# Full-width products of the attention stage issued as four 32-column groups where the array is already tiled

## The chip, the cores and the metric

One core of one Trainium2 chip runs the whole program in one launch. The metric is the device time of that launch in microseconds, the median of the runs shown. All operands are float32.

## What is computed

The input is 8 images of 256 channels by 32 x 32 places. Layer 0 is a convolutional attention, layer 1 is a plain attention and a mixture of 8 experts. Cut to what matters:

```python
# layer 0, on a group-normalised image, 8 heads of 32 channels
q = einsum('bchw,oc->bohw', x, q_w)                  # 1024 queries for each image
k, v = pooled and layer-normed maps of kv_w @ x      # 1426 keys: levels 32x32, 16x16, 11x11, 5x5, each + 3x3 depthwise
out = softmax(q k^T * 32**-0.5) v                    # for each head
x = x + proj_w @ (out mixed by an 8-head global token) + proj_b
# layer 1, on tokens of 256 channels
t = t + softmax((ln(t) Wq)(ln(t) Wk)^T / 16) (ln(t) Wv)
# experts: 8 of them, three products of 256 x 256 each, gates from the mean over the batch
t = t + sum_e gate_e * (relu(bn(relu(bn(ln(t) W1_e)) W2_e)) Wo_e + bo_e)
```

## The kernel before

**Stages.** `attention` does layer 0 and, beside it, layer 1; `experts` does the rest. The attention stage is one loop of 384 steps: 8 images, 2 groups of 4 heads (`c`), 2 halves of the queries and 12 chunks of up to 128 keys (`kc`). The profile shows the first step's scores at about 79 us and the last products at 1970 us.

**One step.** `scores` issues four products of 32 rows, one for each head, which lie in four row groups of TensorE's array and write the four banks of the one buffer `sc`. ScalarE takes the exponential of all 128 x 2048 numbers into `pt` (6 buffers). `values`, for the chunk one step earlier, issues four products whose stationary side is 32 columns wide, in four column groups of the array; they write the four quarters of the partitions of `pv`. In every second step a DMA that accumulates adds one `pt` to another, and VectorE adds such pairs up for the softmax sums; `sums` multiplies them by ones, again in four column groups of 32 (`sm<-pt,con` in the profile).

**Background.** All other work of the stage runs as generators between the steps: key and value maps of the next image (`sm<-xi,kvw`, `sm<-xl,kvw`), queries (`xi,qw`), transposes of keys and values by tokens (`con,acc`, `con,kt`), the projection (`att,mt`), and all of layer 1 (`t,gw`, `y,t`, `wv,t`, `p,v`, sums by `s,con`). Most of these products have a stationary side of 128 x 128 and a moving side of 256, 402 or 512; they write the small buffers `sm` or `sx` of one bank each. After each step's `values`, `f.step((PACE, PACE1))` lets generators put such products on TensorE.

**The order.** `Flow` records every instruction through its `Engine` wrappers. All of them pass through the line `ins = fn(*args, **kwargs)` (L669), which is why the profile has one line for nearly everything and one goes by tiles. Each engine runs strictly in the order of recording. Which generator goes next comes from a planner: `note` adds up a cost for each instruction on a clock for each engine, and `runnable` compares these clocks with the times at which tiles become ready. For TensorE the planner keeps the form of the array in `self.tiled` ("rows", "columns" or None for the full array) and adds an amount to its clock when the form changes:

```python
tiling = None if op == "transpose" else self.tiling(srcs)
if tiling != self.tiled:
    cost += {None: 0.09, "rows": 0.2, "columns": 0.13}[tiling]
    self.tiled = tiling
```

So an ordinary step goes through the array forms rows (`sc`), columns (`pv`), full (background), and again rows.

Of the kernel before, what the change touches and what calls it, by code (L numbers as in the profile page):

```python
# [16 lines left out]
P = 128  # L17
# [3 lines left out]
DH = 32  # L21
# [30 lines left out]
class Kit:  # L52


    def __init__(self, nc):
        self.nc = nc
        self.n = 0
# [80 lines left out]
def chain(*gens):  # L138
    for g in gens:
        yield from g  # L140
# [515 lines left out]
class Flow:  # L656
# [4 lines left out]
    class Engine:  # L661
# [3 lines left out]
        def __getattr__(self, op):  # L665
            fn = getattr(self.eng, op)

            def call(*args, **kwargs):
                ins = fn(*args, **kwargs)  # L669
                self.flow.note(self.name, op, ins, args, kwargs)  # L670
                return ins

            return call

    def __init__(self, tc, kit):
        nc = tc.nc
        self.tc, self.kit = tc, kit
        self.now = dict.fromkeys(("PE", "DVE", "ACT", "POOL", "SP"), 0.0)
        self.last = {}
        self.ready, self.read, self.writer, self.reader, self.slots, self.open = {}, {}, {}, {}, {}, set()  # L680
        self.pe = self.Engine(self, "PE", nc.tensor)
        self.ve = self.Engine(self, "DVE", nc.vector)
        self.act = self.Engine(self, "ACT", nc.scalar)
        self.pool = self.Engine(self, "POOL", nc.gpsimd)
        self.sp = self.Engine(self, "SP", nc.sync)
        self.threads = []
        self.cut = {}
        self.also = {}
        self.tiled = None
        self.credit, self.port = [0.0, 0.0], 0.0  # L690

    def tile(self, pool, shape, tag, bufs=1):
# [18 lines left out]
    def cost(self, engine, op, out, ins):  # L711
# [26 lines left out]
            return 0.14 + 0.00065 * n  # L738
        return 0.15 + 0.00107 * n

    @staticmethod
    def tiling(ins):

        rows, columns = ins[0].shape[0], ins[0].shape[-1]
        return "columns" if columns <= DH and rows > 8 else "rows" if rows == DH else None

    def note(self, engine, op, ins, args, kwargs):
        aps = [a for a in (*args, *kwargs.values()) if hasattr(a, "tensor") or hasattr(a, "space")]
        out = kwargs.get("out", args[0] if args else aps[0])
        srcs = [a for a in aps if a is not out]  # L750
        prev = self.last.get(engine)
        if prev is not None:
            self.tc.add_manual_dep(
                ins.ins,
                prev,
                mybir.DependencyInfo(mybir.DependencyClass.NoSync, mybir.DependencyReason.DATA),
                reason="program order",
            )
        self.last[engine] = ins.ins.name
        start = self.now[engine]  # L760
        names = [n for a in srcs for n in self.keys(a)]
        outs = self.keys(out)
        for n in (*names, *outs):
            if self.writer.get(n) != engine:
                start = max(start, self.ready.get(n, 0.0))
        for o in outs:
            if self.reader.get(o, engine) != engine:
                start = max(start, self.read.get(o, 0.0))
        cost = self.cost(engine, op, out, srcs)
        if engine == "PE":  # L770

            tiling = None if op == "transpose" else self.tiling(srcs)
            if tiling != self.tiled:
                cost += {None: 0.09, "rows": 0.2, "columns": 0.13}[tiling]
                self.tiled = tiling

        wide = [a for a in srcs if a.space != PSUM and a.free_size() > 4]
        if "dma" not in op and engine == "POOL" or engine == "DVE" and wide and (len(wide) > 1 or op in ("tensor_scalar", "tensor_copy")):
            start = max(start, self.port)
            self.port = start + cost  # L780
        self.now[engine] = end = start + cost
        lag = 0.15
        if "dma" in op:
            size = 4e-3 * out.shape[0] * out.free_size() if out.space != DRAM else 4e-3 * srcs[0].shape[0] * srcs[0].free_size()
            lag = 2.0 + 0.0045 * size if engine == "SP" else 1.5 + 0.0078 * size
        for n in {*outs, self.key(out)}:
            self.ready[n] = max(self.ready.get(n, 0.0), end + lag)
            self.writer[n] = "DMA" if "dma" in op else engine
        self.open.difference_update(names)
        for n in {*names, *map(self.key, srcs)}:  # L790
            self.read[n] = max(self.read.get(n, 0.0), end + lag)
            self.reader[n] = engine
# [88 lines left out]
def attention(tc, kit, f, outer, ended, nb, consts, x, t1, t2, hn, bounds, vecs, q_t, kv_t, proj_t, gqk_t, wqk, wqkv, vecs1, w1_d, w1c, gate_d, wrc, vecs2, bnvec):  # L881
# [6 lines left out]
    with ExitStack() as ctx:  # L888
# [5 lines left out]
        def T(pool, shape, tag, bufs=1):  # L894
            return f.tile(pool, shape, tag, bufs=bufs)
# [567 lines left out]
        def scores(b, c, sl, kc):  # L1463
            k0, w = KEY_CHUNKS[kc]
            t = T(psum, [P, 4, 512], "sc")
            for j in range(4):
                r = slice(DH * j, DH * j + DH)
                f.pe.matmul(t[:w, j, :], lhsT=ks[b, c][r, k0 : k0 + w], rhs=qs[b, c][r, sl], start=True, stop=True)
            pt = T(work, [P, 4, 512], "pt", bufs=6)
            f.act.activation(pt[:w], t[:w], AF.Exp, scale=SCALE0)  # L1470
            return pt

        def values(b, c, kc, pt, pv):
            w = KEY_CHUNKS[kc][1]
            for j in range(4):
                h = 4 * c + j
                f.pe.matmul(
                    pv[DH * j : DH * j + DH, :],
                    lhsT=vts[b][kc // 4][:w, kc % 4, h * DH : (h + 1) * DH],
                    rhs=pt[:w, j, :],  # L1480
                    start=kc == 0,
                    stop=kc == NKC - 1,
                )

        def add(kc, pt, into):

            w = KEY_CHUNKS[kc][1]
            f.pool.dma_start(
                out=into[:w].rearrange("p j q -> p (j q)"), in_=pt[:w].rearrange("p j q -> p (j q)"), accum_op=ALU.add
            )  # L1490
# [305 lines left out]
        def unit(b, c, sl, n, pairs):  # L1796
            rec = yield from sums(n, pairs)
            yield from normalise(b, c, sl, rec, n)
            normalised[0] += 1
            if c and sl.start:  # L1800
                f.spawn(project(b), 1)
# [7 lines left out]
        f.finish(lambda: key_parts[0] > 0)  # L1809
        f.spawn(chain(mix(), weights1(), outputs()), 5)  # L1810
        f.spawn(layer1(), 6)
        steps = [(b, c, half, kc) for b in range(nb) for c in range(2) for half in range(2) for kc in range(NKC)]

        pts = {}
        for i in range(len(steps) + 1):
            if i < len(steps):
                b, c, half, kc = steps[i]
                sl = slice(half * 512, half * 512 + 512)
                if kc % 4 == 0:
                    f.finish(lambda: key_parts[0] > 3 * b + kc // 4)  # L1820
                if (half, kc) == (0, 0):
                    f.finish(lambda: (b, c) in qs and (b or (c, 0) in asked))
                    turn[0] = 2 * b + c
                    atts[b, c] = T(work, [P, HW], "att", bufs=2)
                if i == 4:
                    f.finish(lambda: {0, 1}.issubset(whole))
                if b == 0 and kc == 0:
                    f.finish(lambda: (c, half) in asked)
                pts[i] = scores(b, c, sl, kc)
                f.step()  # L1830
            if i:
                b1, c1, half1, kc1 = steps[i - 1]
                if kc1 == 0:
                    pv = T(psum, [P, 512], "pv")
                    pairs = []
                    sl1 = slice(half1 * 512, half1 * 512 + 512)
                    f.spawn(unit(b1, c1, sl1, i // NKC, pairs), 0)
                f.finish(lambda: kc1 // 4 in vts[b1])
                values(b1, c1, kc1, pts[i - 1], pv)
                if kc1 % 2:  # L1840
                    add(kc1, pts.pop(i - 1), pts[i - 2])
                    pairs.append(pts.pop(i - 2))
                if kc1 == NKC - 1:
                    f.finish(lambda: projected[0] >= b1)
                    f.act.activation(atts[b1, c1][:, sl1], pv, AF.Copy)
            if i < len(steps):
                f.step((PACE, PACE1))
        f.finish(lambda: projected[0] == nb)
        f.also.clear()
        f.finish(lambda: f.free("sx") < NEVER)  # L1850
# [683 lines left out]
```

## Time and profile before

| what | us |
|---|---|
| three timed runs | 3314.24, 3327.75, 3323.16 |
| their median | 3323.16 |
| profiled execution, span | 3321.6 |
| TensorE matmuls busy in that span | 3135.7 (94%) |
| weight loads busy | 1914.5 (58%) |
| VectorE busy | 2449.7 (74%) |
| ScalarE busy | 1734.7 (52%) |
| GpSimd busy | 1204.5 (36%) |

The profile gives of its execution the span alone, from the first to the last instruction; this lies 1.6 us under the median of the timed runs. In the groups of instructions `sc<-q,kn 32*128 32x512` reads: the tile `sc` is written from the tiles `q` and `kn`, the stationary side has 32 rows and 128 columns, the moving side is 32 x 512. A float32 product appears as two passes, that is two loads (PEld) and two matmuls (PE). A transpose appears as one. The durations of matmuls overlap and their ends are modelled, so that the distances between starts are the better measure. In the timeline a row is one group of equal instructions: start, length, engine, what, count.

### The profile page before, as it was taken

To read this page: it belongs to the slowest core of one execution; us is meant where nothing else is said; L and a number is where in the kernel's file an instruction comes from. 1 tells how busy PE (TensorE), PEld (TensorE's weight loads), DVE (VectorE), ACT (ScalarE), POOL (GpSimd) and SP (SyncE) were. 2 spreads that over 40 slices of the span, in tenths; PEclk is the share of its full clock that TensorE was granted. 3 is DMA by queue.
4 is the path that set the end of the run, shared out by engine and by line. 5 is a ranking of instruction groups with operands and counts; after the bars stand their busy time and mean duration, and the time that the engine had idled before them with its cause. 6 is when DMAs were issued, how large, how long until landed. Compare 5 with 4: busy or idle time off the path is not lost.

```text
span 3321.6 us, 43017 instructions
## 1 busy us (share of the span) xinstructions
PE 3135.7 (94%) x15970; PEld 1914.5 (58%) x15970; DVE 2449.7 (74%) x4066; ACT 1734.7 (52%) x2328; POOL 1204.5 (36%) x1303
## 2 busy tenths in 40 slices
PE   8687899999999999899899998999999999999997
PEld 4332244344344345345344355777888888888886
DVE  5687788786887886986884555445878887787776
ACT  4476666576576576576566543334333334444442
POOL 2211413213213214213211112006755566777775
PEclk9798999999999999999999999999999999999999
DMA  2357656656646646656556656224444440000000
GB/s 75 84 122 165 125 105 147 130 101 157 130 99 157 138 101 147 137 115 130 125 116 129 143 115 244 73 83 163 142 152 146 146 141 25 20 20 32 20 13 21
DMA packets 112428, 368.09 MB, mean 111 GB/s; under 512 B 13696, under 2 KB 39048, under 8 KB 88976
## 3 DMA queue, kind: packets, MB, share of 16 engines
q0 software_dynamic: 28608, 179.85, 28.2%
q1 hardware_dynamic: 80240, 183.42, 15.9%
q8 instruction: 128, 2.10, 0.3%
q10 hardware_dynamic: 3360, 1.97, 0.2%
q14 instruction: 92, 0.75, 0.1%
HBM read 115.60 MB, written 84.45 MB: 60 GB/s over the span
## 4 chain that ended last, share of the span: by engine, by line
PE 60%; DVE 3%; issue 3%; ACT 2%; DMA 2%; POOL 2%; SPq 0%; DVEq 0%; POOLq 0%; ACTq 0%
PE bank L669 20%; PE sm L669 13%; PE y L669 10%; PE sc L669 6%; PE sx L669 6%; PE pv L669 5%; ACT pt L669 2%; DVE h L669 1%; DMA pt<-pt 1%; DVE u L669 1%; DVE c L669 1%; POOL t L669 0%; ACT h L669 0%; DMA hn<-hn 0%; POOL tm L669 0%
## 5 line engine op out<-in xcount | busy, mean ns | idle before, releaser
L669 ACT ACTIVATE pt<-sc 128x2048 f32<-128x2048 f32 (+1 forms) x384 | 720.2, 1875 | 324.3 <-PE sc L669 270.0
L669 DVE SCALAR_TENSOR_TENSOR acc<-p,vec,acc 128x225 f32<-128x225 f32 (+7 forms) x928 | 527.8, 576 | 29.1 <-ACT acc L669 4.7
L669 PE MATMUL sc<-q,kn 32*128 32x512 f32 (+1 forms) x3072 | 444.7, 649 | 96.5 <-ACT pt L669 95.4
L669 DVE TENSOR_TENSOR pt<-pt,pt 128x1024 f32<-128x1024 f32 x320 | 386.8, 1252 | 142.2 <-DMA pt<-pt 130.3
L669 POOL DMA_DIRECT2D pt<-pt x192 | 174.0, 907 | 778.7 <-ACT pt L669 625.7
L669 PE MATMUL pv<-pt,vt 128*32 128x512 f32 (+1 forms) x3072 | 419.9, 619 | 0.0
L669 ACT ACTIVATE h<-h,bnvec 128x512 f32<-128x512 f32 x456 | 344.9, 805 | 63.8 <-DVE h L669 51.9
L669 ACT ACTIVATE p1c<-bank 128x256 f32<-128x256 f32 x228 | 87.4, 383 | 556.1 <-PE bank L669 538.8
L669 POOL TENSOR_TENSOR rstd<-rstd,mhalf 128x4 f32<-128x4 f32 (+2 forms) x88 | 107.0, 1216 | 672.3 <-DVE rstd L669 618.3
L669 DVE TENSOR_TENSOR h<-p1c,bank 128x512 f32<-128x512 f32 x228 | 155.4, 682 | 213.5 <-PE bank L669 208.3
L669 PEld LDWEIGHTS sc<-q,kn 32*128 32x128 f32 (+1 forms) x3072 | 116.2, 178 | 286.1 <-ACT pt L669 186.0
L669 POOL TENSOR_TENSOR tm<-h,tm 128x256 f32<-128x256 f32 x206 | 239.0, 1160 | 16.2
L669 DVE TENSOR_TENSOR h<-u,bank 128x256 f32<-128x256 f32 x456 | 232.2, 550 | 7.9
L669 PEld LDWEIGHTS pv<-pt,vt 128*32 128x32 f32 (+1 forms) x3072 | 60.8, 108 | 300.7 <-issue 288.4
L669 POOL TENSOR_TENSOR tm<-h 128x512 f32<-128x512 f32 x103 | 134.2, 1303 | 194.3 <-ACT h L669 192.2
L669 DVE TENSOR_TENSOR h<-h,gate 128x1024 f32<-128x1024 f32 x128 | 200.5, 1566 | 1.6 <-DMA h<-h 1.2
L669 PE MATMUL bank<-h,w2e 128*128 128x256 f32 (+1 forms) x612 | 199.0, 454 | 1.9 <-DVE h L669 1.9
L669 PE MATMUL y<-t,s3e 128*128 128x256 f32 x768 | 187.0, 379 | 2.3 <-POOL t L669 2.3
L669 PE MATMUL bank<-t,s1e 128*128 128x256 f32 x750 | 182.4, 379 | 0.0
L669 PE MATMUL sm<-y,t 128*128 128x256 f32 x752 | 180.6, 385 | 0.0
L669 POOL TENSOR_TENSOR t<-h 128x512 f32<-128x512 f32 x106 | 137.3, 1295 | 106.3 <-DVE h L669 87.5
L669 DVE TENSOR_TENSOR u<-h,bank 128x512 f32<-128x512 f32 x228 | 156.8, 688 | 24.2 <-PE bank L669 0.5
(316 smaller groups left out, 5619.2 us busy)
## 6 DMA issues: line engine op xcount, KB each, us to landing
pt<-pt POOLq DMA_DIRECT2D x160, 1024.0 KB, 7.4
h<-h SPq DMA_DIRECT2D x130, 512.0 KB, 3.4
xi<-in_x_dram SPq DMA_DIRECT2D x16, 512.0 KB, 6.3
t<-t SPq DMA_DIRECT2D x8, 1024.0 KB, 9.3
res<-t SPq DMA_DIRECT2D x32, 256.0 KB, 3.9
t<-res SPq DMA_DIRECT2D x32, 256.0 KB, 4.6
hn<-res SPq DMA_DIRECT2D x32, 256.0 KB, 2.9
hn<-hn SPq DMA_DIRECT2D x16, 512.0 KB, 4.7
```

The costliest lines, as they stand in the source:

```text
L669: ins = fn(*args, **kwargs)
```

## The change

While the attention loop runs (`f.columns`), a matmul whose stationary side is 128 x 128 and whose moving side has at least 128 columns is issued as four matmuls, each with 32 columns of the stationary side, the whole moving side, and 32 partitions of the output, if the instruction recorded last on TensorE left the array in rows or columns. Transposes do not pass through this branch, stay full width, and set the form to full, so that products which follow a transpose stay full width as well until the next tiled product. The planner's amount for going to the full array changes from 0.09 to 0.2. The rest of the kernel is as it was.

```diff
@@ Flow.Engine.__getattr__
-            return call
+            if op != "matmul":
+                return call
+
+            def product(out, lhsT, rhs, **kwargs):
+                if not self.flow.narrow(lhsT, rhs):
+                    return call(out, lhsT=lhsT, rhs=rhs, **kwargs)
+                for j in range(0, P, DH):
+                    call(out[j : j + DH], lhsT=lhsT[:, j : j + DH], rhs=rhs, **kwargs)
+
+            return product
@@ Flow.__init__
         self.tiled = None
+        self.columns = False
@@ Flow
+    def narrow(self, lhsT, rhs):
+
+        return self.columns and self.tiled is not None and tuple(lhsT.shape) == (P, P) and rhs.free_size() >= P
@@ Flow.note
             if tiling != self.tiled:
-                cost += {None: 0.09, "rows": 0.2, "columns": 0.13}[tiling]
+                cost += {None: 0.2, "rows": 0.2, "columns": 0.13}[tiling]
                 self.tiled = tiling
@@ attention
         f.spawn(layer1(), 6)
+        f.columns = True
         steps = [(b, c, half, kc) for b in range(nb) for c in range(2) for half in range(2) for kc in range(NKC)]
...
             if i < len(steps):
                 f.step((PACE, PACE1))
+        f.columns = False
         f.finish(lambda: projected[0] == nb)
```

## The prediction

> **What bounds the kernel now.** I read first the page's busy shares and slices, then the table by stretches of time, then TensorE's waits, and last its timeline inside the attention stage.
>
> ```profile
> PE 3135.7 (94%) x15970; PEld 1914.5 (58%) x15970; DVE 2449.7 (74%) x4066; ACT 1734.7 (52%) x2328; POOL 1204.5 (36%) x1303
> ...
> PE   8687899999999999899899998999999999999997
> ```
>
> One row of the table by stretches, then the first row of TensorE's waits (us in total, times, longest):
>
> ```profile
> 480.00:760.00 280.00, 270.20 (x1526) 125.62 (x1526) 227.23 (x394) 179.02 (x221) 66.51 (x75) 0.99 0.58 125
> ```
>
> ```profile
> PE sc L669 <- ACT pt L669: 95.4, 95, 3.3
> ```
>
> TensorE is busy nearly everywhere. In the stretch from 480 to 760 us (columns: PE, PEld, DVE, ACT, POOL busy, then clock, DMA share, GB/s) it is busy for 96.5% at a clock of 0.99; VectorE follows at 81%, ScalarE at 64%. The only wait of size is `sc` for the exponential, 95 us in 95 places. Going through the 383 steps of the loop, 67 of the 68 steps with neither background product nor transpose wait there, and of the 265 steps that hold a full-width background product 245 hold no TensorE wait at all. So a step with background work is as long as its TensorE work, and the question is what TensorE spends there beside streaming. TensorE's timeline (start, length, count of records):
>
> ```profile
> 682.21 1.14 PE L669 MATMUL sc<-q,kn 32*128 32x512 f32 x8
> 683.28 1.06 PE L669 MATMUL pv<-pt,vt 18*32 18x512 f32 x8
> 684.27 1.62 PE L669 MATMUL sm<-xl,kvw 128*128 128x402 f32 x4
> 685.73 1.89 PE L669 MATMUL sm<-wv,t 128*128 128x256 f32 x8
> 687.55 1.14 PE L669 MATMUL sc<-q,kn 32*128 32x512 f32 x8
> 688.62 1.06 PE L669 MATMUL pv<-pt,vt 128*32 128x512 f32 x8
> 689.62 0.66 PE L669 MATMUL sx<-con,acc 128*128 128x128 f32 x4
> 690.11 1.04 PE L669 MATMUL sm<-con,acc 128*128 128x128 f32 x8
> 691.08 1.14 PE L669 MATMUL sc<-q,kn 32*128 32x512 f32 x8
> 692.15 1.07 PE L669 MATMUL pv<-pt,vt 128*32 128x512 f32 x8
> 693.03 1.04 PE L669 MATMUL sx<-pt,con 128*32 128x512 f32 x8
> 694.00 1.09 PE L669 MATMUL sm<-con,acc 128*128 128x128 f32 x8
> ...
> 703.18 1.99 PE L669 MATMUL sx<-y,t 128*128 128x256 f32 x8
> 705.10 1.14 PE L669 MATMUL sc<-q,kn 32*128 32x512 f32 x8
> ```
>
> Read the distances between starts; over the whole stage they repeat within a few ns, and I give the medians.
> - **Leaving columns.** `pv` takes 0.996 us when a full-width group follows (688.62 to 689.62) and 0.883 when another column group follows (692.15 to 693.03): 0.113 us for the switch.
> - **Entering full.** Eight passes of 256 take 1.924 us to the next `sc` after `pv` (703.18 to 705.10) and 1.820 after another full-width group (685.73 to 687.55): 0.104 us. Transposes pay less: four take 0.492 after `pv` (689.62 to 690.11), 0.437 after a full-width group: 0.055.
> - **Leaving full.** Full-width passes of 256 follow each other every 0.216 us, eight are 1.728, so 1.820 holds 0.092 for the switch to rows.
> - **Streaming is the same in both forms.** A pass of 512 takes 0.429 us full width, and four column groups together take 0.429 for each of their passes (`sx<-pt,con`). Splitting neither saves nor adds streaming, if all four run side by side.
>
> **What the Trainium skill says.** "TensorEngine Tiling (Array Packing)", Key Properties: changing the tiling mode, not just the tile, drains the engine. The trace agrees: 0.09 to 0.11 us for each leaving. The same page, Restrictions, rules out float32 transposes under column tiling; the trace shows them at 128*128 alone, so the switches around them stay. "TensorE: Matmul & The Clock Gate", LDWEIGHTS: a load takes its columns divided by 1.2, in ns, so 107 ns for 128 and 27 for 32. The trace agrees: successive loads of 128 start 107 ns apart, which is the 0.104 of entering, and the first pass of `pv` is 25 ns longer than its later ones.
>
> **The change part by part.** *What is split.* In the changed program's order of TensorE instructions 1178 products are split: 852 with 256 moving columns, 54 with 402, the others with 512 (four of the 256s lie behind the last `sc`). That is 3534 more matmuls, each two loads and two matmul records. No other engine gets an instruction for it; 382 switches from rows to columns stay.
>
> *Switches that vanish and that come.* Counted in the two orders (before, after), groups of columns with few rows taken as columns:
> - columns to full 240, 10, at 0.113 + 0.104: 52.1 and 2.2 us
> - full to rows 243, 33, at 0.092: 22.4 and 3.0
> - columns to transposes 76, 92, at 0.113 + 0.055: 12.8 and 15.5
> - columns to rows 72, 281, at 0.113: 8.1 and 31.8
>
> The sum falls from 95.4 to 52.5 us, **by 43 us**. For one ordinary step: 0.113 + 0.104 + 0.092 before, 0.113 after, so 0.196 us of 3.99.
>
> *What of it is on the path.* Nearly all, as 245 of 265 steps are TensorE's alone. In the other 20 (7.5%) the gain only makes a wait longer: 3.2 us back. A dense step falls from 3.99 to 3.79 us and stays above the 3.14 us of a step that waits for ScalarE.
>
> *Splitting itself.* The trace before has no column group with 256 moving columns. From below: no cost, as in `sx<-pt,con` after `pv`, whose loads are under way while `pv` still streams; a gain is excluded because the passes already stream at full rate. From above: each product shows its first 32-column load, 0.025 us x 1178 = 29 us. I take nothing; the cover is the pass before, 216 ns long against four loads of 27.
>
> *The planner.* The new amounts change the order on every engine. Of small-buffer work, 5.6 us of TensorE time moves from behind the last `sc` into the stage; work only moved costs nothing on a bound engine. In the experts stage 104 instead of 112 products of 512 and 14 more of 256 stand on TensorE: 8 x 0.858 less 14 x 0.432, 0.9 us less. Which steps get which products is reshuffled; steps that wait now lose 134 us in all in the loop, and I allow 8 us either way for that. The `pt` transfers on GpSimd's queue (7.4 us to land) get a step 5% shorter; VectorE waits for them 120 us today, and late ones would show as ScalarE waiting for a `pt` buffer, today 22 us.
>
> Sum: 3321.6 - 43.0 + 3.2 - 0.9 = 3280.9 us for the profiled execution. It stood 1.6 us under the median, so **3283 us** (-1.2%).
>
> **The rivals.**
> *Issue cannot keep up (slower).* A split 256-wide pass needs four load-and-matmul pairs in 216 ns, one each 54 ns; before it was one each 216. With R ns for a pair, each such pass takes 4R where 4R exceeds 216. The gain of 43 us is gone at 852 x 2 x (4R - 216) = 43 us, R = 60 ns, and the kernel is slower by over 0.5% from R = 63 on. The densest chain before (`sc`, `pv`, `sx<-pt,con`: 24 pairs in 2.9 us) is one pair each 122 ns, set by streaming, so a sustained rate in question is not shown. "TensorE: Matmul & The Clock Gate", Back-to-back issue gap, gives 81 ns as sustained for such pairs at 128 columns: then 1704 x 108 ns = 184 us more, less 43, **3464 us**. Against it: that figure is for loads of 128 columns, and in one column group the records of the four pairs start 7 ns apart, which needs them waiting in the queue, but also says that they are accepted that fast. Also the blocks of 256 instructions (16 KB each) come in 0.9 to 1.5 us by the queue's packets, while a block will last 7 us at the densest. Chance 7%.
>
> *Another resource takes half.* The exponential, the `pt` transfers or VectorE (83% busy after) end more steps, or the loads of each product show: gain 43 - 21, **3302 us**. For it: 120 us of VectorE waits for `pt`. Against it: these waits lie beside a busy TensorE. Chance 12%, of which 5% within 0.5%.
>
> *The change does little, as the planner's order spends the gain*: 3318 us. Against it: the counts above are of the order as built. Chance 2%.
>
> **How the numbers follow.** About 0.5% (17 us) is what a measurement of this kernel can tell from no change, so faster means under 3306. The forecast has 79%, the rivals as above. Faster: 79 + 7 = 86%; same: 5 + 2 = 7%; slower 7%. Range: the upper bound of the unknown split cost (3283 + 29 = 3312) and the half-gain case lie below 3312; the lower end allows 8 us for order and as much for steps now waiting that close up: 3267.
>
> **What would show it.** In the changed profile, `pv` to the next column group at 0.88 us instead of 1.00, a split group of four 256-wide products (32 records) to the next `sc` at 1.73 + 0.11 = 1.84 instead of 1.92, dense steps of 3.79 us; and the wait of `sc` for the exponential at 90 to 105 us. The forecast is wrong if split passes of 256 come further apart than 0.216 us (issue), if each product's first pass is 25 ns longer (loads), or if the wait of `sc` grows by over 20 us (ScalarE or `pt`).

## The result, and the profile after

The changed kernel takes 3309.0 us (median of 11 runs, 3303.4 to 3317.9), the kernel before 3322.1 us (11 runs). The ratio is 0.9965, 95% interval 0.9954 to 0.9975: 13 us or 0.35% faster, where 40 us were forecast.

The page of the changed kernel, the lines of the span, the busy times and the slices:

```profile
span 3308.1 us, 57168 instructions
...
PE 3098.8 (94%) x23038; PEld 1790.7 (54%) x23038; DVE 2455.2 (74%) x4068; ACT 1733.4 (52%) x2330; POOL 1217.1 (37%) x1315
...
PE   8687899999999999999899889999999999999997
```

There are 7068 more matmul records, which is 2 for each of the 3534 added instructions, and TensorE's busy time falls by 37 us. The row of the table for the stretch from 480 to 760 us, then the first row of TensorE's waits:

```profile
480.00:760.00 280.00, 268.01 (x2740) 107.84 (x2736) 232.95 (x402) 180.29 (x230) 66.47 (x77) 0.99 0.58 126
```

```profile
PE sc L669 <- ACT pt L669: 105.8, 106, 4.7
```

The same stretch of time now holds 2740 records at the same clock, VectorE has gone from 81 to 83%, and the wait of `sc` for the exponential has grown by 10 us. TensorE's timeline in the loop (start, length, count):

```profile
697.80 0.66 PE L669 MATMUL sx<-con,acc 128*128 128x128 f32 x4
698.29 1.04 PE L669 MATMUL sm<-con,acc 128*128 128x128 f32 x8
699.26 1.14 PE L669 MATMUL sc<-q,kn 32*128 32x512 f32 x8
700.33 1.06 PE L669 MATMUL pv<-pt,vt 128*32 128x512 f32 x8
701.22 1.91 PE L669 MATMUL sx<-y,t 128*32 128x256 f32 x32
702.94 1.91 PE L669 MATMUL sm<-y,t 128*32 128x256 f32 x32
704.78 1.14 PE L669 MATMUL sc<-q,kn 32*128 32x512 f32 x8
705.85 1.06 PE L669 MATMUL pv<-pt,vt 128*32 128x512 f32 x8
706.74 1.91 PE L669 MATMUL sm<-y,t 128*32 128x256 f32 x32
708.58 1.14 PE L669 MATMUL sc<-q,kn 32*128 32x512 f32 x8
```

This is what the prediction said of an ordinary step (0.88, 1.84, 3.79), within a hundredth. `pv` to the next group is 0.89 us, 32 records of a split group take 1.72 when another follows (701.22 to 702.94) and 1.84 up to `sc` (706.74 to 708.58), and the step from 704.78 to 708.58 is 3.80 us. The transposes around 698 us cost what they did. So each switch that vanished paid its price, and 27 us are missing elsewhere.

**Where they went, from the traces.** I divide the loop (start of the first `sc` to the start of the last one) into TensorE's idle time, the streaming of the background products (counts times the durations of the prediction), and the rest (scores, values, switches, and what a slower clock adds):

| us | before | changed |
|---|---|---|
| start of the loop | 78.6 | 80.3 |
| loop | 1887.4 | 1873.0 |
| of it idle | 133.6 | 150.4 |
| of it background streaming | 845.6 | 851.2 |
| of it the rest | 908.2 | 871.4 |
| after the loop | 1355.6 | 1354.8 |

The rest falls by 37 us, near the forecast 43. Against it stand 17 us more idle time and 6 us of work moved into the loop. The time after the loop does not give this work back in these two traces: its TensorE busy time falls by 6.6 us, its idle time rises by 5.9. Whether the idle time comes from the new order or from faster steps, these two traces cannot say.

### The profile page after: what moved, and what is told of

Its sections match the earlier page's. It is cut to its first block, busy times and chain, and to the rows that moved or that the text cites. A ratio compares the mean times of both kernels' runs of the same rounds, so it can differ in the third digit from the quotient of the medians.

```text
span 3308.1 us, 57168 instructions
## 1 busy us (share of the span) xinstructions
PE 3098.8 (94%) x23038; PEld 1790.7 (54%) x23038; DVE 2455.2 (74%) x4068; ACT 1733.4 (52%) x2330; POOL 1217.1 (37%) x1315
## 5 line engine op out<-in xcount | busy, mean ns | idle before, releaser
L669 PE MATMUL sm<-p,v 128*32 128x256 f32 (+1 forms) x2416 | 192.3, 379 | 0.7 <-ACT p L669 0.7
L669 POOL TENSOR_TENSOR t<-h,t 128x256 f32<-128x256 f32 x216 | 172.9, 800 | 17.0
```

## The experiments

The split and the planner's new accounts come together in the change. The first four runs take them apart: theory A blames the new order for the missing time, theory B the faster steps themselves.

### The split in the old order

The planner keeps its old amounts and accounts one full-width product, while four column groups are issued. Every engine's order is that of the kernel before, apart from the splitting; a second state, `form`, follows the array.

```diff
+            def product(out, lhsT, rhs, **kwargs):
+                flow = self.flow
+                if not flow.narrow(lhsT, rhs):       # asks form instead of tiled
+                    return call(out, lhsT=lhsT, rhs=rhs, **kwargs)
+                for j in range(0, P, DH):
+                    ins = fn(out[j : j + DH], lhsT=lhsT[:, j : j + DH], rhs=rhs, **kwargs)
+                    if j + DH < P:
+                        flow.follow(self.name, ins)  # program order alone
+                flow.note(self.name, op, ins, (out,), dict(lhsT=lhsT, rhs=rhs, **kwargs))
+                flow.form = "columns"
```

> The same products are split into four column groups, but the planner keeps the costs and the state that it has before the change, so that every engine's order of work is that of the kernel before. Theory A (the split earns what the switches cost, about 40 us, and the changed order of the planner spends 27 of it): 0.9877 of before, about 3282 us, with the loop's TensorE idle time at about 135 us as before. Theory B (the shorter steps meet ScalarE and the transfers of pt in any order, so that only a third is left): 0.996 of before, about 3309 us, idle time in the loop at 150 us or more.

Measured: 3304.7 us, 0.9955 of before (0.9941 to 0.9970), 16 us. Theory A's 3282 falls: with the old order kept, more than half of the forecast gain is missing too. B's mechanism is not confirmed as it stands either: the loop's idle time is 141 us, above A's 135 but short of B's 150. What else is missing is taken up below.

### The new order at full width

The planner's accounts are those of the changed kernel, with four notes for each product, but one full-width matmul is issued.

```diff
-                for j in range(0, P, DH):
-                    call(out[j : j + DH], lhsT=lhsT[:, j : j + DH], rhs=rhs, **kwargs)
+                ins = fn(out, lhsT=lhsT, rhs=rhs, **kwargs)
+                for j in range(0, P, DH):
+                    part = dict(lhsT=lhsT[:, j : j + DH], rhs=rhs, **kwargs)
+                    self.flow.note(self.name, op, ins, (out[j : j + DH],), part)
```

> The order of the changed kernel on every engine, with the planner's accounts as after the change, but each product is issued full width. Theory A: the order itself costs 27 us and the switches come back, 1.008 of before, about 3349 us. Theory B: the order is as good as the old one, 1.000 of before, about 3322 us.

Measured: 3334.2 us, 1.0039 of before (1.0026 to 1.0052). The new order costs 13 us at full width, half of what A needs and more than B allows. In its profile the loop is 17 us longer than before, with 8 us more idle time and 6 us more background work; the time after the loop is 6 us shorter. In this order the split earns 25 us (3334 to 3309), in the old order 16. So both are at work.

### The planner's amount by itself

The changed kernel with the amount for the full array left at 0.09 (its edit is shown), and the kernel before with it raised to 0.2:

```diff
-                cost += {None: 0.2, "rows": 0.2, "columns": 0.13}[tiling]
+                cost += {None: 0.09, "rows": 0.2, "columns": 0.13}[tiling]
```

> The changed kernel, with the planner's amount for going to the full array left at 0.09: a third order, between the other two in what the planner knows. Theory A: orders differ by some 10 to 30 us by chance, so anything from 3280 to 3312 us, and the difference to the changed kernel lies in waits of TensorE and work left for after the loop. Theory B: 3309 us within 5, as the order does not matter.

> The kernel before, with only the planner's amount changed from 0.09 to 0.2; no product is split. Theory A: another order, which by itself moves the time by some 10 to 30 us either way: 3300 to 3350 us. Theory B: 3322 us within 5.

Measured: 3346.3 us (1.0079 of before, 1.0065 to 1.0093) and 3351.3 us (1.0096, 1.0081 to 1.0110). Both lie beyond the ranges that I gave for A. One constant of the planner moves the kernel before by 30 us and the changed kernel by 37, more than the change does. In the changed kernel with the old amount the loop holds 177 us of TensorE idle time against 134 before. In the kernel before with the new amount, 17 us less background streaming is in the loop, and the time after it is 1377 us against 1356.

### What stops the faster steps: GpSimd's queue

The kernel before and the split in the old order have the same steps in the same order, so the starts of their steps can be compared one by one. Between images the gain builds up at about 1.4 us for each 12 steps, the forecast's rate (43 us over 384 steps). But 21 steps are longer than before, by 23 us together, mostly at the same places of each image. One of them: GpSimd's timeline of the split in the old order.

```profile
633.42 0.93 POOL L669 DMA_DIRECT2D pt<-pt  x1
...
642.84 2.57 POOL L669 TENSOR_TENSOR rstd<-rstd,mhalf 128x8 f32<-128x8 f32 x1 [7.84 <-DVE rstd L669]
645.37 0.89 POOL L669 DMA_DIRECT2D pt<-pt  x1
```

ScalarE's timeline of the same time:

```profile
633.09 1.88 ACT L669 ACTIVATE pt<-sc 128x2048 f32<-128x2048 f32 x1 [2.85 <-PE sc L669]
...
644.67 1.88 ACT L669 ACTIVATE pt<-sc 128x2048 f32<-128x2048 f32 x1 [1.26 <-PE sc L669]
652.49 1.88 ACT L669 ACTIVATE pt<-sc 128x2048 f32<-128x2048 f32 x1 [5.95 <-DMA pt<-pt]
```

Counting two exponentials for each of these DMAs, the one at 645.37 adds the pair whose second exponential is done at 635.0. It is issued 10.4 us later, because a small power (an elementwise `pow`) for layer 1's norm stands ahead of it in GpSimd's queue, and this waits 7.8 us for VectorE. From 646.5 on ScalarE has no free `pt` buffer, it waits 5.95 us for the transfer, and then TensorE waits for ScalarE. The kernel before has the same stop, at 4.92 us:

```profile
662.21 1.88 ACT L669 ACTIVATE pt<-sc 128x2048 f32<-128x2048 f32 x1 [4.92 <-DMA pt<-pt]
```

So the split did not make this stop; it made it 1.03 us longer, and the step with it 1.02. When the stop ends depends on when VectorE lets the power go, so a gain that TensorE made before it can be lost there. A seventh `pt` buffer would be the plain test; the memory of the stage has no room for it. Instead these powers are issued only when their reader, or another GpSimd computation, comes. Accumulating DMAs thus move ahead of them; the planner's accounts and every other engine's order stay.

```diff
-            f.pool.tensor_tensor(out, out, kit.mhalf[: out.shape[0], 0:1].to_broadcast(out.shape), ALU.pow)
+            f.later(out, kit.mhalf[: out.shape[0], 0:1].to_broadcast(out.shape))
...
+        if engine == "POOL" and "dma" not in op or any(self.key(out) in names for out, _ in self.powers):
+            for out, half in self.powers:
+                self.follow("POOL", self.kit.nc.gpsimd.tensor_tensor(out, out, half, ALU.pow))
+            self.powers.clear()
```

> As e1_old_order_split, but GpSimd's small power instructions (rstd) are issued only when their reader or another GpSimd computation comes, so that accumulating transfers of pt no longer stand behind a power that waits for VectorE. All other engines keep their order. Theory C (the split's gain is given back in a few places for each image, where a pt transfer stands in GpSimd's queue behind such a wait, the six pt buffers run out, ScalarE and then TensorE stop, and TensorE's clock falls to half): 15 to 30 us under e1, 3275 to 3290 us, and ScalarE's wait for pt transfers falls from 26 to under 10 us. Rival D (the transfers themselves are late because they share the DMA engines with others): within 5 us of e1, 3300 to 3310 us.

> The kernel before with the same deferral of the powers, no product split. Theory C: the same stalls exist before and cost some 22 us of ScalarE's waiting; 10 to 25 us under before, and the split (e6 against this one) then earns 25 to 40 us instead of 16. Rival D: within 5 us of before, the split earns 16 us again.

> The changed kernel with the same deferral. Theory C: 10 to 25 us under the changed kernel, 3285 to 3300 us. Rival D: within 5 us of it, 3309 us.

| medians, us | full width | split | split earns |
|---|---|---|---|
| old order | 3319.8 to 3322.1 | 3304.7 | 16 |
| old order, powers deferred | 3314.7 | **3282.7** | 32 |
| new order | 3334.2 | 3309.0 | 25 |
| new order, powers deferred | not run | 3296.5 | |

Against the kernel before the three new ones stand at 0.9885 (0.9865 to 0.9904), 0.9982 (0.9974 to 0.9989) and 0.9926 (0.9909 to 0.9944). Theory C holds for the interplay at the medians: deferring the powers earns 5 us at full width, below C's range and no more than D allowed, and 22 us with the split in the old order; D's "within 5 us" falls for both split kernels. In the profiled executions the interplay is smaller. There the deferral shortens the loop by 17 us with the split (10 us of idle time and 7 of lost clock, which the next section explains) and by 9 us at full width (9 and 2). The profiled execution of the deferred full-width kernel took 3320.6 us, 6 above its median, so the two ways of counting cannot be brought closer here. The rows of ScalarE's waits for `pt` transfers between 80 and 1960 us (total, times, longest), the split in the old order without the deferral and then with it:

```profile
ACT pt L669 <- DMA pt<-pt: 26.5, 9, 5.9
```

```profile
ACT pt L670 <- DMA pt<-pt: 13.0, 7, 3.2
```

The wait halves and does not fall under 10 as I had written; the 5.95 us above are gone. GpSimd's timeline of the deferred kernel around the same step shows the same transfer ahead of the power, 0.5 us after its exponential (done at 636.2):

```profile
636.67 0.91 POOL L670 DMA_DIRECT2D pt<-pt  x1 [1.34 <-ACT pt L670]
644.70 2.55 POOL L791 TENSOR_TENSOR rstd<-rstd,mhalf 128x8 f32<-128x8 f32 x1 [7.12 <-DVE rstd L670]
```

The split in the old order with the powers deferred is the fastest kernel of the study: 1.15% under the kernel before, and under the changed kernel by 26 us.

### What a longer wait costs beside itself: the clock

Another of the 21 longer steps, first in the kernel before (TensorE's timeline):

```profile
786.76 1.07 PE L669 MATMUL pv<-pt,vt 128*32 128x512 f32 x8
789.78 0.38 PE L669 MATMUL sm<-mv,con 128*128 128x2 f32 x2 [1.96 <-DVE res L669]
790.09 1.14 PE L669 MATMUL sc<-q,kn 32*128 32x512 f32 x8
791.16 1.07 PE L669 MATMUL pv<-pt,vt 128*32 128x512 f32 x8
```

and in the split in the old order:

```profile
773.38 1.06 PE L669 MATMUL pv<-pt,vt 128*32 128x512 f32 x8
777.73 0.59 PE L669 MATMUL sm<-mv,con 128*128 128x2 f32 x2 [3.29 <-DVE res L669]
778.24 2.09 PE L669 MATMUL sc<-q,kn 32*128 32x512 f32 x8
780.26 1.93 PE L669 MATMUL pv<-pt,vt 128*32 128x512 f32 x8
```

TensorE comes early and waits 3.29 instead of 1.96 us for VectorE. VectorE's work up to `res` runs without a pause from the landing of a `pt` transfer on and takes 11.8 us in both kernels (777.94 to 789.73, and 765.89 to 777.68), so it does not shorten with TensorE's steps. The deferral leaves this wait as it is (3.40 us). After it `sc` takes 2.09 us instead of 1.14 and `pv` 1.93 instead of 1.07. The rows by stretches (last three columns: granted clock, DMA share, GB/s) show TensorE's clock; the kernel before around its wait, then the split kernel around its own:

```profile
785.00:790.00 5.00, 3.04 (x20) 0.69 (x18) 4.65 (x8) 3.77 (x5) 0.93 (x2) 1.00 1.03 210
```

```profile
775.00:785.00 10.00, 7.27 (x38) 3.58 (x38) 5.55 (x11) 4.74 (x5) 0.98 (x2) 0.66 0.95 211
```

The Trainium skill has this in "TensorE: Matmul & The Clock Gate", Part 1: after an idle window of about 3.4 us the clock is halved, until it has been busy as long. The traces agree in part. Half clock comes in pieces of 3.4 us: here the clock record has half speed for 6.8 us from 777.3 on, which costs 3.4 us and is the 0.66 over 10 us. Over the loops of all nine kernels, the 63 pauses of TensorE of 3 us or more all have half clock beside them: it begins during the pause or within 3.5 us of its end, or (9 of them) was there already. But of the pauses between 1.5 and 3 us over half were followed by it too: the 1.96 us above left the clock at 1.00, while 1.92 us at 638.4 in the kernel before were followed by 3.4 us of half clock. The pauses of 3.2 to 3.4 us cost 1.7 or 3.4 us of clock, and up to 5.1 us in the first image. So the length of a single pause does not decide it alone.

Over the loop these records add up to 51 us of lost clock before and 61 for the split in the old order; with the deferral to 49 at full width and 54 with the split; in the new order to 51 both at full width and with the split (the changed kernel). The cost of the clock is read from the records; no run takes it away by itself.

For three pairs of the same order the profiled loops can be added up (us; the switches counted in each order at the prediction's prices):

| pair | switches less | more idle | more lost clock | loop shorter | unassigned |
|---|---|---|---|---|---|
| old order | 41.5 | 7 | 10 | 22 | 2 |
| old order, powers deferred | 41.5 | 6 | 5 | 29.5 | 1 |
| new order | 42.5 | 9 | 0 | 31 | 2.5 |

Of the 31 us of the new order the medians show 25: in its profiles the time after the loop, where nothing is split, is 5 us longer with the split. With the powers deferred it is 5 us shorter, so of the 32 us between the medians some may not be the split's.

## Why the prediction was wrong

- **The switches** (43 us): right, in kind and size. The steps of the timeline came out at 0.89, 1.84 and 3.80 us for the predicted 0.88, 1.84 and 3.79. (Two slips of reading change nothing: successive loads of 128 columns stand 108 to 110 ns apart in the trace, not 107, and the 0.9 us of the experts stage is 0.8.)
- **Splitting itself, taken at nothing**: right. Split passes of 256 follow each other at 0.216 us, with one load-and-matmul pair each 54 ns, and no product shows its first load: the first pass of a split group after `pv` is as long as the later ones, 0.216 us. The rival of issue did not occur.
- **"What of it is on the path: 3.2 us back"**: this step failed. It took a step without a wait for one that stays TensorE's when everything gets faster, and compared its 3.79 us with ScalarE's 3.14 alone. But waits on other engines that are set by VectorE's chain do not shorten; TensorE only comes to them earlier. In place of 3.2 us the same-order pairs show 6 to 9 us more idle time and up to 10 us of lost clock, of which the forecast had nothing; at the medians, the split earned 16 us in the old order and 25 in the new, not 40. That some of this hangs on GpSimd's queue, where a `pt` transfer stands behind a waiting power, is shown by the deferral: it brings the split from 16 to 32 us in the old order (from 22 to 29.5 in the profiled loops). The rest, as the wait for `res`, is read from the traces and has no run of its own. I had named the `pt` transfers as the place to look, with 120 us of VectorE waiting for them, and then argued that these waits lie beside a busy TensorE. I did not read GpSimd's queue, where such powers already stood before the change: the one in the example waited 8.5 us there.
- **"I allow 8 us either way" for the planner's order**: a mis-sized term. The new order costs 13 us at full width, 4 with the split (3304.7 to 3309.0, which noise does not tell from nothing) and 14 with the split and the powers deferred (3282.7 to 3296.5). So about half of the missing 27 us is the order's and the rest what the split itself did not earn. One changed constant costs 30 to 37. The rival that the order spends the gain had 2%, far too little, and was dismissed because the counts were "of the order as built": they counted switches, not waits.
- **The half-gain rival** (3302 us, waits of ScalarE or `pt`) is what came nearest. Its mechanism is in part the right one, with the order's cost on top; but its sign, the wait of `sc` growing by over 20 us, did not show (10 us). That the measured time lies near its number is partly luck, as the order's cost fills the gap.
- **Work moved into the loop** was said to cost nothing. In the changed kernel's profile it cost about what was moved, 6 us, since idle time after the loop grew by as much. The same order at full width shows no such cost (1349.6 us after the loop against 1355.6 before), so why it arose is open.

## What to carry to other kernels

A switch of the array's form is worth its drain and its first load, about 0.2 us for each visit to the full array here, and splitting into column groups took it away at no cost in streaming for moving sides of 256. How much arrives depends on the waits that other engines set: walk through the places where the bounding engine waits already, and ask of each whether it will end earlier; if not, the gain made before it is lost, and a wait that grew past 3 us had half clock beside it in every place of these runs. Where a planner orders the work, build the new order without the new instructions: here it cost 13 us, as much as the change earned.

## What the runs showed of the hardware that was not expected

Column groups accept a weight load and a matmul each 54 ns for as long as 64 records in a row (701.22 to 704.78), and four pairs start within 20 ns of each other when they wait in the queue. A GpSimd power on 128 x 8 numbers takes 2.2 us in the mean of 8 (2.57 in the example), longer than the 0.9 us of the DMA issue that it holds up, and its own wait holds that DMA up too. And a wait of 3.3 us on TensorE can cost as much again in clock as it lasts.
